# Mixture-of-experts groups: VectorE turns squares two groups ahead, TensorE turns the first group, and gates are chosen in front of outputs

## The chip, the cores and the metric

The kernel runs on one core of a Trainium2 chip. The metric is the device time of one execution in microseconds, the median of several. A core has TensorE for matrix products, VectorE, ScalarE and GpSimd for everything else on chip, and SyncE, which here does nothing but issue transfers. The profile calls them PE, DVE, ACT, POOL and SP, and TensorE's loading of a stationary operand PEld. Each engine has its own list of instructions and works through it in order; engines wait for each other by semaphores.

## The reference

All numbers are fp32. A graph layer (a 4096 by 4096 adjacency matrix times features) is followed by a causal attention layer with four heads of 64, and then by the experts, which are what the change touches:

```python
x = x + y @ wo.T
flat = _rmsnorm(x, ln2_w).reshape(-1, Cx)            # 4096 tokens of 256
probs = jax.nn.softmax(flat @ router_w.T, axis=-1)   # 8 experts
tp, ti = jax.lax.top_k(probs, TOPK)                  # 2 for each token
tp = tp / (jnp.sum(tp, axis=-1, keepdims=True) + 1e-09)
weights = jnp.sum(tp[..., None] * jax.nn.one_hot(ti, NE, dtype=flat.dtype), axis=1)
out = jnp.zeros_like(flat)
for e in range(NE):
    hh = jax.nn.silu(flat @ w1[e].T) * (flat @ w3[e].T)   # 682 hidden units
    out = out + weights[:, e:e + 1] * (hh @ w2[e].T)
return x + out.reshape(Bx, Tx, Cx)
```

## The kernel before, in words

The graph layer takes the first third of the span and attention the second. While attention still runs, a router picks two experts for each token and writes the token's row (normalised values, its place in the output, its gates) into lists in DRAM, one stretch for each expert. The expert stage starts at about 1027 us. It works through 42 groups of listed tokens, each belonging to one expert. A group is *whole* (256 tokens) or *small* (128 tokens). `TURNS` gives the order: turns 0 to 8 are whole; from 9 on small and whole mostly alternate, but small follows small at turns 15 and 16, 24 and 25, 31 and 32, and a whole one comes behind each of these pairs; the last two turns are whole.

**Inputs.** TensorE needs the tokens with their 256 features on partitions, so the listed rows must be transposed. `load_squares(k)` (issues at L1426) does part of that by DMA: four transfers, one for each quarter of the partitions, put 32 by 32 squares in place. `prepare(k)` does the rest: VectorE transposes inside squares (L1443), and ScalarE scales by the norm's weights into `xT` (L1448, one instruction for each half of the features). VectorE then also forms four sums of the inputs for a group that needs them (`sums_x`, L1512), and picks the gate of each token from its row (L1455 and L1460), which came by a transfer of its own (`load_rows`, L1433).

**Products.** For a small group, and for whole groups up to turn 10, `hidden` forms the hidden units in steps of `q`: products (L1728), silu on ScalarE (L1734), multiplication on VectorE (L1735). After the first step it calls `prepare` for the next turn. For whole groups from turn 12 to 39, `hidden_seven` forms the same in the manner of Strassen, with seven products of half-sized blocks in place of eight (L1558). Its banks A, B and D of PSUM are copied out by ScalarE (L1564) and added to by VectorE (L1567), first for most chunks (`one`), then for the rest (`two`); a bank that was just copied is written again by a later product, S2 by T2 after S1 by T1. It calls `prepare` for the next turn near its end, and then multiplies (L1596 and L1597) and forms sums of the hidden units (`split`, L1645 to L1648). The sums of its input weights are made by GpSimd in the turn before (`sums13`, L1491 to L1494 and on).

**Outputs.** `combine(k)` runs one turn late, inside turn k + 1 and behind that turn's hidden units. It multiplies by the second weight matrix: plainly for small groups (L1779), by seven products for whole groups from turn 4 on (`seven_products`, L1688), which need sums of the weights (`sums2`, L1664 to L1667, on VectorE; made ahead where a whole group follows a small one) and a recombination on VectorE (L1696 to L1702). ScalarE multiplies by the gate (L1790), and GpSimd adds the rows into the output by an indirect transfer (L1801).

**What sets the order.** The loop over turns is written out by hand: hidden units of k; sums of weights for k + 1 if due; outputs of k − 1; then GpSimd sets `sent` (L1937) and SP writes it to DRAM (L1938), which holds SP's queue behind the outputs; then SP issues `load2(k + 4)` (L1403), `load13(k + 5)` (L1397), the squares and the rows of k + 4. Loads of the first groups are issued from inside attention (`begin_experts`), and `prepare(0)` stands in the list of attention's last steps, before its last value products (L827) and beside its last row sums (L813).

Of the kernel before, what the change touches and what calls it, by code (L numbers as in the profile page):

```python
# [66 lines left out]
def fast_kernel(  # L67
# [618 lines left out]
    with (  # L686
# [668 lines left out]
        def entry(t, most):  # L1355
            return nc.values_load(
                t, engines=[SP], min_val=0, max_val=most,
                skip_runtime_bounds_check_because="the lists are as long as the tokens are many",
            )
# [25 lines left out]
            at2 += (pt_all[:, at + 2 * W13 : at + 2 * W13 + W2],)  # L1385
        w13s = [a.rearrange("p (c w) -> p c w", c=2) for a in at13]
        w2s = [a.rearrange("p (k c) -> p k c", k=NF + 1) for a in at2]
        rows, hidden_of, inputs_of, expert_of, gates_of, rows_at = {}, {}, {}, {}, {}, {}


        def halves(i):
            return HALF if i < NW else 1

        def load13(k):
            i = TURNS[k]
            expert_of[i] = entry(table[0:1, 1, i : i + 1], NE - 1)
            nc.sync.dma_start(  # L1397
                w13s[k % 5], w13[bass.ds(expert_of[i], 1)].rearrange("o p c w -> p (o c) w")
            )
# [8 lines left out]
        def loaded(i, get):  # L1408
            if i < NA:
                free(get, "late writes", "the rows of the first groups are whole by then")  # L1410
                join(get, "first reads")

        def squares_room(k):
            return late[:, LATE_Z + k % 5 * 2 * C : LATE_Z + (k % 5 + 1) * 2 * C]

        def load_squares(k):

            i = TURNS[k]
            n = halves(i)
            at = rows_at[i] = entry(  # L1420
                table[0:1, 0, i : i + 1], NE * REG - (GR if i < NW else 0)
            )
            z = squares_room(k)[:, 0 : n * C].rearrange("p (m e) -> p m e", e=2 * Q)
            tokens = lists[bass.ds(at, n * P), 0:C].rearrange("(m i) (g e) -> g i m e", i=Q, g=4)
            for g in range(4):
                loaded(i, nc.sync.dma_start(z[g * Q : (g + 1) * Q], tokens[g]))  # L1426

# [8 lines left out]
            ))  # L1436
            rows[i] = r

        def prepare(k):
            i = TURNS[k]  # L1440
            n = halves(i)
            turned = squares_room(k + 4)[:, 0 : n * C]
            nc.vector.transpose(turned, squares_room(k)[:, 0 : n * C])  # L1443
            turned = turned.rearrange("p (m c i) -> p c m i", c=2, i=Q)
            xT = late[:, LATE_XT + k % 2 * 2 * GR : LATE_XT + k % 2 * 2 * GR + 2 * n * P]
            xT = xT.rearrange("p (c i) -> p c i", c=2)
            for c in range(2):
                nc.scalar.activation(  # L1448
                    xT[:, c, :].rearrange("p (m i) -> p m i", i=Q), turned[:, c], AF.Copy, scale=ln2_sb[:, c : c + 1]
                )  # L1450
            inputs_of[i] = xT
            if k in SPLIT13:
                sums_x(k, turned)
            pick = ex.tile([P, n, NE], F32, tag="pick", name=f"pick_{i}")
            nc.vector.tensor_mul(  # L1455
                pick, rows[i][:, 0:n, 1:KEPT],
                mine[:, i : i + 1, :].to_broadcast([P, n, NE]),
            )
            gates_of[i] = ex.tile([P, n, 1], F32, tag="gt", name=f"gt_{i}", bufs=3)
            nc.vector.tensor_reduce(gates_of[i], pick, AX.X, ALU.add)  # L1460

# [57 lines left out]
        def hidden_seven(k, step, behind):  # L1519
# [46 lines left out]
            def added(dst, q, bank):  # L1566
                nc.vector.tensor_add(dst, dst, bank[:, 0 : len(q.chunks), :])  # L1567
# [10 lines left out]
                copied(q.u2, q, q.A)  # L1578
                product(q, q.D, "S4", "B22")

            def added_up(q):
                added(q.s1, q, q.B)
                added(q.u2, q, q.D)

            def third(q):
# [15 lines left out]
            sums2(k)  # L1601
            begun(one)
            second(one)
            added_up(one)
            step()
            begun(two)
            third(one)
# [9 lines left out]
            third(two)  # L1617
            step()
            if behind is not None:
                prepare(behind)  # L1620
            gated(two)
            si = ax.tile([P, GR], F32, tag="rden", name=f"si_{i}_t")
            nc.scalar.activation(si[T0 : T0 + TAIL, :], tail[0:TAIL, :], AF.Silu)
# [81 lines left out]
        def hidden(k, step=None, behind=None):  # L1705
            i = TURNS[k]
            n = halves(i) * P
            w13_sb, xT = w13s[k % 5], inputs_of.pop(i)
            hT = hTs[k % 2][:, :, 0:n]
            for q in range(0, NF + 1, 2):  # L1710
                if not p_h:
                    pool = next(p_sc)
                    if pool is p_sc1:
                        ps = [
                            pool.tile([P, 2, GR], F32, tag="sc", name=f"h_{i}_{q}_{m}")
                            for m in range(2)
                        ]
                    else:
                        ps = pool.tile([P, 2, 2, GR], F32, tag="sc", name=f"h_{i}_{q}")
                        ps = [ps[:, m] for m in range(2)]  # L1720
                else:
                    ps = [
                        p_h[0].tile([P, 2, GR], F32, tag="h", name=f"h_{i}_{q}_{m}")[:, :, 0:n]
                        for m in range(2)
                    ]
                for m in range(2 * q, min(2 * q + 4, 2 * NF + 1)):
                    for c in range(2):
                        nc.tensor.matmul(  # L1728
                            ps[m % 2][:, m // 2 - q, :], w13_sb[:, c, m * P : (m + 1) * P],
                            xT[:, c, :], start=(c == 0), stop=(c == 1),  # L1730
                        )
# [3 lines left out]
                nc.vector.tensor_mul(  # L1735
                    hT[:, q : q + both, :], si[:, 0:both, :], ps[1][:, 0:both, :]
                )
                if q == 0 and behind is not None:
                    prepare(behind)
                if step and q < NF - 1:  # L1740
                    step()

            nc.scalar.activation(si[T0 : T0 + TAIL, 1, :], ps[0][0:TAIL, 1, :], AF.Silu)
            nc.vector.tensor_mul(
                hT[T0 : T0 + TAIL, NF, :], si[T0 : T0 + TAIL, 1, :], ps[0][T0 : T0 + TAIL, 1, :]
            )
            hidden_of[i] = hT
            if k in SEVEN:
                split(k, hT)

        def combine(k):
# [2 lines left out]
            w2_sb = w2s[k % 5]  # L1754
            hT = hidden_of.pop(i)
            r = rows.pop(i)
            gt = gates_of.pop(i)
            if k < ALONE or k % 2:
                y = ax.tile([P, HALF, C], F32, tag="yT1", name=f"y_{i}")
            else:  # L1760
# [52 lines left out]

        def begin_experts():
            make_table(NB - 1, True, 0, NA)
            load13(0)
            load_squares(0)
            load_squares(1)
            load2(0)
            load13(1)  # L1820
            for k in range(2):
                load_rows(k)
            load_squares(2)
            load2(1)
            load_squares(3)
            for k in range(2, 4):
                load_rows(k)
# [39 lines left out]
        for b in ORDER[:-1]:  # L1867
# [7 lines left out]
            lambda: give_back([("late", n) for n in range(4)])  # L1875
        )
        later.setdefault(PLACES - 2, []).append(
            lambda: [prepare(0)] + [nc.gpsimd.memset(t[:, NF, :], 0.0) for t in hTs]
        )

        scored = 0
# [31 lines left out]
        load13(3)  # L1913
        load2(3)
        load13(4)
        for k in range(NM):
            if k == 3:
                sc_scope.close()
                p_h.append(ctx_h.enter_context(tc.tile_pool(name="e_h", bufs=6, space=PSUM)))
            if k == NM - 1:  # L1920


                between = iter([lambda: None, lambda: combine(k - 1)])
            if k in SPLIT13:
                hidden_seven(k, step, k + 1)
            else:
                hidden(
                    k, step if k < NM - 1 else lambda: next(between)(),
                    k + 1 if k + 1 < NM else None,
                )  # L1930
            step()
            if k + 1 in SPLIT13 and TURNS[k] >= NW:
                sums2(k + 1)
            if 0 < k < NM - 1:
                combine(k - 1)
                if k + 4 < NM:
                    nc.gpsimd.memset(sent, 0.0)  # L1937
                    nc.sync.dma_start(sent_dram, sent)  # L1938
            if k + 4 < NM:
                load2(k + 4)  # L1940
            if k + 5 < NM:
                load13(k + 5)
            if k + 4 < NM:
                load_squares(k + 4)
                load_rows(k + 4)
            if 0 < k < NM - 1:
                step()
                if k >= ALONE and TURNS[k - 1] < NW:
# [746 lines left out]
```

## Time and profile before

| | us |
|---|---|
| median of 3 runs | 1547.53 (1547.2 to 1548.44) |
| profiled execution, device time | 1541.6 |
| its span | 1539.8 |
| adjacency and attention products in it, L532 and L785 | 370.4 and 282.3 busy |
| first expert product | at 1032.0 |
| mean granted TensorE clock | 0.997 |

The span is what the profiler saw from the first to the last instruction. The profiled execution lies 5.9 us below the median, so places in it are compared among themselves, and differences, not totals, are carried over to the median. A wait is listed by the engine that waited, its line, what released it, and then total us, number, and longest. In a timeline line the first number is the start in us, the second the length, and brackets hold the idle time of the engine just before and what ended it; lengths of consecutive equal instructions are lumped and their number given as x.

Times of single operations, as far as the change touches them, all from the same execution:

| operation | us each |
|---|---|
| turn, L1443, small and whole | 0.44 and 0.70 |
| scaling, L1448, two of a small and two of a whole group | 0.69 and 0.91 |
| pick, L1455, mean of 42 (alone: 0.17) | 0.466 |
| gate, L1460, mean | 0.166 |
| one input sum, L1512, mean | 0.50 to 0.58 |
| small output, L1790 | 0.47 |

### The profile page before, as it was taken

Reading aid. Unit: us, or ns where it says so; the run is one execution under the profiler, and the core shown is the slowest. Engines: PE = TensorE matmul, PEld = TensorE weight load, DVE = VectorE, ACT = ScalarE, POOL = GpSimd, SP = SyncE. Lnnn points to the kernel's source line nnn. Section 1 sums busy time; section 2 is a strip of 40 time slices with the busy share of each in tenths; the row PEclk is TensorE's granted clock in tenths of the full one; section 3 lists DMA queues with packets and bytes.
Section 4 is the critical chain, followed back from the end, with each engine's and each line's share of the span. In section 5 each row is a group of like instructions: output and inputs, shape, how many; then the busy total and the mean of one; then the engine's idle time right before and its main releaser. Section 6 shows DMA issues by size and latency. Waiting matters only on the chain.

```text
span 1539.8 us, 28601 instructions
## 1 busy us (share of the span) xinstructions
PE 1509.4 (98%) x10791; PEld 1113.9 (72%) x10791; DVE 1085.2 (70%) x2224; ACT 554.4 (36%) x989; POOL 556.6 (36%) x649
## 2 busy tenths in 40 slices
PE   9999999999999999999999999989999999999987
PEld 8888888888888543444444434448899899999986
DVE  7864665755655667878878978875676787787872
ACT  2102012021021456565665565643123333333331
POOL 2102022122221331374554643442424545545342
PEclk9999999999999999999999999999999999999999
DMA  6344444543544000011011011059878798898955
GB/s 239 131 132 153 154 140 147 173 146 124 174 142 149 5 1 29 15 58 36 29 51 36 33 33 37 22 164 293 221 213 229 225 271 242 234 282 232 265 118 133
DMA packets 106590, 212.19 MB, mean 138 GB/s; under 512 B 63466, under 2 KB 82922, under 8 KB 92810
## 3 DMA queue, kind: packets, MB, share of 16 engines
q1 hardware_dynamic: 92906, 192.00, 38.7%
q0 software_dynamic: 12720, 17.47, 6.4%
q8 instruction: 87, 1.43, 0.4%
q10 hardware_dynamic: 816, 0.79, 0.2%
q14 instruction: 61, 0.50, 0.1%
HBM read 184.48 MB, written 27.13 MB: 137 GB/s over the span
## 4 chain that ended last, share of the span: by engine, by line
PE 93%; DMA 2%; DVE 2%; issue 1%; POOL 1%; ACT 0%; SPq 0%; DVEq 0%; POOLq 0%; ACTq 0%
PE acc L532 25%; PE sc L785 14%; PE h L1728 13%; PE y_second L827 5%; PE y_third L827 4%; PE y_first L827 4%; PE ye_y L1779 4%; PE hA L1558 4%; PE ye_y L1688 3%; PE ye_ms L1688 2%; PE pq L612 2%; PE pf L503 2%; PE hD L1558 2%; PE ph L193 2%; PE po L913 1%
## 5 line engine op out<-in xcount | busy, mean ns | idle before, releaser
L785 PE MATMUL sc<-qT_all,kT 64*64 64x512 f32 (+3 forms) x2304 | 282.3, 557 | 0.5 <-ACT pt_all L793 0.3
L532 PE MATMUL acc<-a,g 128*128 128x256 f32 x1024 | 244.1, 380 | 0.0
L532 PEld LDWEIGHTS acc<-a,g 128*128 128x128 f32 x1024 | 193.9, 190 | 31.5 <-issue 6.7
L785 PEld LDWEIGHTS sc<-qT_all,kT 64*64 64x64 f32 x2304 | 91.3, 133 | 128.5 <-issue 109.1
L793 ACT ACTIVATE pt_all<-sc 128x1024 f32<-128x1024 f32 (+3 forms) x157 | 148.7, 954 | 96.8 <-PE sc L785 94.4
L1801 POOL DMA_INDIRECT acc_dram<-y,late x40 | 63.1, 1577 | 185.0 <-ACT y L1790 121.3
L532 PE MATMUL acc<-more_sums,g 128*128 128x256 f32 x512 | 126.3, 380 | 0.0
L813 DVE TENSOR_TENSOR late<-late,pt_all 128x1024 f32<-128x1024 f32 (+3 forms) x91 | 106.7, 1173 | 24.3 <-POOL pt_all L795 9.9
L1728 PE MATMUL h<-late,qT_all 128*128 128x256 f32 (+1 forms) x616 | 106.7, 333 | 4.6 <-ACT late L1448 4.6
L433 ACT COPY qT_all<-tr 128x512 f32<-128x512 f32 x30 | 16.2, 588 | 259.5 <-PE tr L431 259.5
L532 PEld LDWEIGHTS acc<-more_sums,g 128*128 128x128 f32 x512 | 97.4, 190 | 13.0
L827 PE MATMUL y_first<-pt_all,vv 64*64 64x512 f32 (+3 forms) x448 | 106.6, 554 | 0.0
L1728 PEld LDWEIGHTS h<-late,qT_all 128*128 128x128 f32 x616 | 95.4, 194 | 15.0 <-ACT late L1448 5.4
L625 POOL TENSOR_TENSOR rot<-rot,tables 128x512 f32<-128x512 f32 x21 | 34.1, 1626 | 198.6 <-ACT rot L621 158.4
L827 PE MATMUL y_second<-pt_all,vv 64*64 64x512 f32 (+3 forms) x436 | 104.2, 555 | 0.0
L1075 POOL DMA_INDIRECT lists<-row,slots x64 | 88.3, 1379 | 17.6 <-issue 15.1
L827 PE MATMUL y_third<-pt_all,vv 64*64 64x512 f32 (+3 forms) x372 | 88.8, 555 | 0.0
L621 ACT ACTIVATE rot<-pq 32x512 f32<-32x512 f32 x84 | 49.4, 588 | 82.7 <-DVE qT_all L619 43.7
L1735 DVE TENSOR_TENSOR late<-si,h 128x256 f32<-128x256 f32 (+2 forms) x87 | 39.0, 465 | 56.9 <-ACT si L1734 38.8
L1734 ACT ACTIVATE si<-h 128x256 f32<-128x256 f32 (+2 forms) x87 | 34.7, 413 | 93.2 <-PE h L1728 90.4
L813 DVE TENSOR_TENSOR sum_all<-sum_all,pt_all 128x1024 f32<-128x1024 f32 (+3 forms) x51 | 56.0, 1098 | 15.8 <-POOL pt_all L795 9.5
L793 ACT ACTIVATE late<-sc 128x1024 f32<-128x1024 f32 (+3 forms) x55 | 50.9, 927 | 41.4 <-PE sc L785 38.0
(489 smaller groups left out, 3347.0 us busy)
## 6 DMA issues: line engine op xcount, KB each, us to landing
a<-in_adj_dram SPq DMA_DIRECT2D x64, 1024.0 KB, 4.9
qT_all<-in_w_dram SPq DMA_DIRECT2D x18, 1408.0 KB, 10.0
pt_all<-in_w_dram SPq DMA_DIRECT2D x16, 1408.0 KB
res_all<-in_w_dram SPq DMA_DIRECT2D x17, 768.0 KB, 5.5
pt_all<-in_w_dram SPq DMA_DIRECT2D x16, 768.0 KB, 5.5
res_all<-in_w_dram SPq DMA_DIRECT2D x8, 1408.0 KB, 6.2
qT_all<-in_w_dram SPq DMA_DIRECT2D x9, 768.0 KB, 5.5
late<-lists SPq DMA_DIRECT2D x100, 64.0 KB, 8.7
```

The source lines that it names most:

```text
L532: nc.tensor.matmul(acc[bank][:, at, :], g[jb][:, right, k, :], m[left][:, k, :], start=(jb == 0 and k == 0 and at == 0), stop=(jb == NB - ...
L621: nc.scalar.activation(rot[n * Q : (n + 1) * Q, :], pj[(n ^ 1) * Q : ((n ^ 1) + 1) * Q, :], AF.Copy, scale=1.0 if n % 2 else -1.0,)
L785: nc.tensor.matmul(ps[k * HP : (k + 1) * HP, j, :w], kT[sb][hd, i * P + k * HP : i * P + (k + 1) * HP], qT[b][hd, p, off:], start=True, st ...
L793: nc.scalar.activation(pt[:, :, :w], ps[:, :, :w], AF.Exp, scale=HD ** -0.5)
L813: nc.vector.tensor_add(sums[b, p][:, :, off:], before[:, :, off:], pt[:, :, : 512 - off])
L827: nc.tensor.matmul(accs[b, p][k][hd, off:], vv[sb][some, i, hd], pt[some, j, : 512 - off], start=(s == order_of(b)[0]), stop=(s == order_o ...
L1075: put = nc.gpsimd.indirect_dma_start(out=lists[:, :], out_offset=bass.IndirectOffsetOnAxis(ap=chosen[b][:, k, t, :], axis=0), in_=flats[b] ...
L1558: nc.tensor.matmul(bank[:, n, :], m[left][:, c, :], m[right], start=first and n == 0, stop=True, skip_group_check=True,)
L1688: nc.tensor.matmul(p[number], m[left][:, j, :], m[right][:, j, :], start=(n % 4 == 0 and j == 0), stop=(j == 2), skip_group_check=True,)
L1728: nc.tensor.matmul(ps[m % 2][:, m // 2 - q, :], w13_sb[:, c, m * P : (m + 1) * P], xT[:, c, :], start=(c == 0), stop=(c == 1),)
L1779: nc.tensor.matmul(ps[h if last else 0][:, h, :], hT[:, q, cols], w2_sb[:, q, :], start=(q == 0), stop=(q == NF),)
L1801: put = nc.gpsimd.indirect_dma_start(out=(acc_dram if k < NM - LAST else out)[:, :], out_offset=at, in_=y[:, h, :], in_offset=None, comput ...
```

## The change

Three edits, and what follows from them.

First, the inputs of turn 0. `load_tokens(0)` fetches the 256 rows in one transfer of whole rows, ahead of the first weights on SP. `begin_inputs` takes the place of `prepare(0)`: ScalarE reorders each half of the tokens, TensorE transposes four 128 by 128 blocks into a PSUM bank, and ScalarE scales these into `xT`.

Second, `prepare` is taken apart. `turn(k)` is VectorE's transpose; `turns_in` lists in which turn each is done. A whole group turns the squares of the next turn and, if that is small, those of the turn after it too. In `hidden_seven` the first stands before VectorE's first bank addition of `one` and the second between its two; in `hidden` they stand after the first step. Only where small follows small does a small group turn for its successor. `scale_inputs(k)` is ScalarE's part; a small group whose successor is already turned does it at its very start. Squares are loaded one turn earlier, and those of turn 4 ahead of the loop.

Third, picking the gates moves out of `prepare(k)` into the start of `combine(k)`, in front of the output that it scales. On VectorE it so stands behind the split and the weight sums of the turn in which the outputs are formed.

```diff
+        def load_tokens(k):
+            n = halves(TURNS[k])
+            get = nc.sync.dma_start(
+                squares_room(k)[:, 0 : n * C].rearrange("p (h c) -> p h c", c=C),
+                lists[bass.ds(place_of(TURNS[k]), n * P), 0:C].rearrange(
+                    "(h p) c -> p h c", p=P
+                ),
+            )
+            loaded(TURNS[k], get)
...
-        def prepare(k):
+        def begin_inputs():
+            n = halves(TURNS[0])
+            listed, tokens = (
+                squares_room(at)[:, 0 : n * C].rearrange("p (h c) -> p h c", c=C)
+                for at in (0, 4)
+            )
+            for h in range(n):
+                nc.scalar.copy(in_groups(tokens[:, h]), in_order(listed[:, h]))
+            tr = p_ms.tile([P, 2, n, P], F32, tag="ms", name="tx")
+            for h in range(n):
+                for c in range(2):
+                    nc.tensor.transpose(
+                        tr[:, c, h, :], tokens[:, h, c * P : (c + 1) * P], ident
+                    )
+            xT = room_for_inputs(0)
+            for c in range(2):
+                nc.scalar.activation(
+                    xT[:, c, :], tr[:, c].rearrange("p h i -> p (h i)"), AF.Copy,
+                    scale=ln2_sb[:, c : c + 1],
+                )
+
+        turned_of, turns_in = {}, {}
+        for k in range(1, NM):
+            alone = TURNS[k - 1] < NW or TURNS[k - 2] >= NW
+            turns_in.setdefault(k - 1 if alone else k - 2, []).append(k)
+
+        def turn(k):
+            n = halves(TURNS[k])
+            turned = squares_room(k + 4)[:, 0 : n * C]
+            nc.vector.transpose(turned, squares_room(k)[:, 0 : n * C])
+            turned_of[k] = turned.rearrange("p (m c i) -> p c m i", c=2, i=Q)
...
+        def gates(k, r):
...
-            def added_up(q):
+            def added_up(q, behind=()):
+                behind = iter(behind)
+                for j in behind:
+                    turn(j)
+                    break
                 added(q.s1, q, q.B)
+                for j in behind:
+                    turn(j)
                 added(q.u2, q, q.D)
...
-            added_up(one)
+            added_up(one, turns_in.pop(k, []))
...
-                prepare(behind)
+                scale_inputs(behind)
+                if behind in SPLIT13:
+                    sums_x(behind, turned_of.pop(behind))
...
+            early = behind in turned_of
+            if early:
+                scale_inputs(behind)
             for q in range(0, NF + 1, 2):
...
                 if q == 0 and behind is not None:
-                    prepare(behind)
+                    for j in turns_in.pop(k, []):
+                        turn(j)
+                    if not early:
+                        scale_inputs(behind)
+                    if behind in SPLIT13:
+                        sums_x(behind, turned_of.pop(behind))
...
-            gt = gates_of.pop(i)
+            gt = gates(k, r)
...
+            load_tokens(0)
             load13(0)
-            load_squares(0)
             load_squares(1)
...
-            lambda: [prepare(0)] + [nc.gpsimd.memset(t[:, NF, :], 0.0) for t in hTs]
+            lambda: [begin_inputs()] + [nc.gpsimd.memset(t[:, NF, :], 0.0) for t in hTs]
...
+        load_squares(4)
...
             if k + 4 < NM:
-                load_squares(k + 4)
+                if k + 5 < NM:
+                    load_squares(k + 5)
                 load_rows(k + 4)
```

More of the change, by code (lines that the diff above doesn't have):

```diff
@@ L1387, in fast_kernel @@
         w2s = [a.rearrange("p (k c) -> p k c", k=NF + 1) for a in at2]
-        rows, hidden_of, inputs_of, expert_of, gates_of, rows_at = {}, {}, {}, {}, {}, {}
+        rows, hidden_of, inputs_of, expert_of, rows_at = {}, {}, {}, {}, {}
         def halves(i):
@@ L1414, in squares_room, with place_of @@
             return late[:, LATE_Z + k % 5 * 2 * C : LATE_Z + (k % 5 + 1) * 2 * C]
+        def place_of(i):
+            if i not in rows_at:
+                rows_at[i] = entry(
+                    table[0:1, 0, i : i + 1], NE * REG - (GR if i < NW else 0)
+                )
+            return rows_at[i]
+        def load_tokens(k):
[7 more added lines that the diff above has]
+            loaded(TURNS[k], get)
         def load_squares(k):
@@ L1419, in load_squares @@
             n = halves(i)
-            at = rows_at[i] = entry(
-                table[0:1, 0, i : i + 1], NE * REG - (GR if i < NW else 0)
-            )
-            z = squares_room(k)[:, 0 : n * C].rearrange("p (m e) -> p m e", e=2 * Q)
-            tokens = lists[bass.ds(at, n * P), 0:C].rearrange("(m i) (g e) -> g i m e", i=Q, g=4)
+            z = squares_room(k)[:, 0 : n * C].rearrange("p (m e) -> p m e", e=2 * Q)
+            tokens = lists[bass.ds(place_of(i), n * P), 0:C].rearrange(
+                "(m i) (g e) -> g i m e", i=Q, g=4
+            )
             for g in range(4):
@@ L1437, in load_rows, with room_for_inputs @@
             rows[i] = r
-        def prepare(k):
+        def room_for_inputs(k):
+            n = halves(TURNS[k])
+            xT = late[:, LATE_XT + k % 2 * 2 * GR : LATE_XT + k % 2 * 2 * GR + 2 * n * P]
+            inputs_of[TURNS[k]] = xT.rearrange("p (c i) -> p c i", c=2)
+            return inputs_of[TURNS[k]]
+        def begin_inputs():
[17 more added lines that the diff above has]
+                    scale=ln2_sb[:, c : c + 1],
+                )
@@ new lines, in fast_kernel, with scale_inputs @@
+        turned_of, turns_in = {}, {}
[3 more added lines that the diff above has]
+        def turn(k):
+            n = halves(TURNS[k])
+            turned = squares_room(k + 4)[:, 0 : n * C]
+            nc.vector.transpose(turned, squares_room(k)[:, 0 : n * C])
+            turned_of[k] = turned.rearrange("p (m c i) -> p c m i", c=2, i=Q)
+        def scale_inputs(k):
+            xT = room_for_inputs(k)
+            for c in range(2):
+                nc.scalar.activation(
+                    xT[:, c, :].rearrange("p (m i) -> p m i", i=Q), turned_of[k][:, c],
+                    AF.Copy, scale=ln2_sb[:, c : c + 1],
+                )
@@ L1440, in prepare @@
+        def gates(k, r):
             i = TURNS[k]
             n = halves(i)
[L1442 to L1450, printed above, removed]
@@ L1451, in prepare @@
-            inputs_of[i] = xT
-            if k in SPLIT13:
-                sums_x(k, turned)
             pick = ex.tile([P, n, NE], F32, tag="pick", name=f"pick_{i}")
             nc.vector.tensor_mul(
-                pick, rows[i][:, 0:n, 1:KEPT],
+                pick, r[:, 0:n, 1:KEPT],
                 mine[:, i : i + 1, :].to_broadcast([P, n, NE]),
             )
-            gates_of[i] = ex.tile([P, n, 1], F32, tag="gt", name=f"gt_{i}", bufs=3)
-            nc.vector.tensor_reduce(gates_of[i], pick, AX.X, ALU.add)
+            gt = ex.tile([P, n, 1], F32, tag="gt", name=f"gt_{i}", bufs=3)
@@ L1465, in fast_kernel @@
+            nc.vector.tensor_reduce(gt, pick, AX.X, ALU.add)
+            return gt
         SEVEN = [k for k in range(4, NM - 2) if TURNS[k] < NW]
```

## The prediction

> **What bounds the kernel now.** I read the head of the page first, then its chain of work that ended last.
>
> ```profile
> span 1539.8 us, 28601 instructions
> PE 1509.4 (98%) x10791; PEld 1113.9 (72%) x10791; DVE 1085.2 (70%) x2224; ACT 554.4 (36%) x989; POOL 556.6 (36%) x649
> PE 93%; DMA 2%; DVE 2%; issue 1%; POOL 1%; ACT 0%; SPq 0%; DVEq 0%; POOLq 0%; ACTq 0%
> ```
>
> TensorE is busy 98% of the span. The diff adds four TensorE instructions and takes none away, so it can win only by filling TensorE's gaps. The view of waits, for TensorE from 1000 us on, lists them:
>
> ```profile
> PE hA L1558 <- issue: 12.6, 7, 2.1
> PE h L1728 <- ACT late L1448: 4.6, 1, 4.6
> PE hA L1558 <- DVE hy L1567: 1.2, 1, 1.2
> ```
>
> That is 18.4 us in nine gaps: one of 4.6 at the first expert group, eight of 1.2 to 2.1 later. The timeline at the first:
>
> ```profile
> 1026.87 0.60 PE L827 MATMUL y_second<-pt_all,vv 64*64 64x512 f32 x2
> ...
> 1029.05 1.75 DVE L813 TENSOR_TENSOR sum_all<-sum_all,pt_all 128x256 f32<-128x256 f32 x2
> ...
> 1030.72 0.70 DVE L1443 STREAM_TRANSPOSE late<-late 128x512 f32<-128x512 f32 x1
> 1031.46 0.91 ACT L1448 ACTIVATE late<-late,ln_sb 128x256 f32<-128x256 f32 x2 [6.73 <-DVE late L1443]
> ...
> 1032.02 6.42 PE L1728 MATMUL h<-late,qT_all 128*128 128x256 f32 x16 [4.56 <-ACT late L1448]
> ```
>
> The inputs wait for VectorE's turn, and that stands behind attention's last sums. The windows give, after the times, busy us of PE, PEld, DVE, ACT, POOL, then granted clock, DMA share and GB/s:
>
> ```profile
> 1032.00:1034.00 2.00, 1.98 (x5) 1.61 (x6) 0.00 (x0) 1.98 (x3) 0.00 (x0) 0.50 0.98 366
> 1034.00:1036.00 2.00, 2.00 (x6) 1.56 (x5) 0.00 (x0) 0.14 (x1) 0.00 (x0) 0.50 1.28 168
> 1050.00:1100.00 50.00, 50.00 (x235) 44.08 (x234) 23.53 (x76) 14.69 (x33) 24.75 (x40) 1.00 0.86 248
> 1200.00:1250.00 50.00, 47.93 (x386) 46.68 (x387) 37.33 (x85) 18.50 (x48) 28.13 (x30) 1.00 0.81 223
> ```
>
> After the long gap TensorE runs at half clock until about 1037; the early whole groups then have no gap at all; the mixed stretch has short ones. One of those, group 14 (whole) behind 13 (small):
>
> ```profile
> 1206.05 1.49 DVE L1455 TENSOR_TENSOR pick<-late,mine 128x8 f32<-128x8 f32 x1
> ...
> 1213.61 0.42 DVE L1735 TENSOR_TENSOR late<-si,h 128x256 f32<-128x256 f32 x1
> ...
> 1221.26 0.29 DVE L1700 TENSOR_TENSOR vv<-vv,ye_ms 128x128 f32<-128x128 f32 x1
> ...
> 1221.58 1.02 ACT L1790 ACTIVATE wo_sb<-vv,gt 128x256 f32<-128x256 f32 x2 [4.78 <-DVE vv L1700]
> 1222.51 0.57 ACT L1564 COPY qT_all<-hA 128x512 f32<-128x512 f32 x1
> 1223.18 1.13 PE L1558 MATMUL hA<-kT,res_all 128*128 128x128 f32 x8 [1.99 <-issue]
> ```
>
> The releaser reads "issue", but the order on ScalarE tells it: the copy of bank A (1222.51) is queued behind an output (1221.58) that waits for VectorE's recombination, and the next product into A cannot start before it. VectorE's chain, not TensorE, sets the pace of such a pair: 23.1 us between equal points where it stalls, 20.87 where it does not.
>
> [...] 0.50 after 4.56 us idle, 1.00 after gaps of 2.0. [...] The pick above takes 1.49 us beside GpSimd's weight sums and 0.17 away from them; the transpose keeps 0.44 beside them.
>
> **The change part by part.** *Start.* Removed: four loads of squares and the 0.70 turn behind VectorE's sums. Added: one token load, two ScalarE copies, four TensorE transposes. The token load goes to SP ahead of group 0's w13. I expect tokens by 1023. ScalarE's last exponential ends at 1024.73; two copies of about 0.42 (from the scale, half of 0.91) end at 1025.6. The transposes stand before the last value products. No such row exists; [...] fp32 128x128 products here follow each other at 0.11. I take 0.16 each, 0.66 in all [...]. They and the last products end by 1027.6, and ScalarE's scaling by 1027.6. w13(0), issued 1.2 us later, should land near 1027.5 instead of 1026.2; it could be 1028.7 if the token load is held by the last scatter. First product at 1027.8 instead of 1032.0: −4.2. [...] sixteen products take 3.45 (as a warm set at 1046.71) instead of 6.42: −2.97. The denominators' products need sum_all (1030.8), which TensorE reaches at 1031.2: covered; w13(1) lands at 1037 to 1039, needed at 1039.3: covered, just. I allow +0.2. **Start −7.0** (−4 to −7.5).
>
> *Turns moved.* A whole group now turns one or two squares (0.44 and 0.70) where VectorE idles, 1.05 and 1.51 us by its waits, before and between its bank additions. Those gaps are the cover; without it each turn costs its own length. Squares are loaded one turn earlier: still four issues per group on SP, in the same place of its order (ahead of the rows, behind w13), with one set more up front, behind w13(4). The DMA share of 0.8 leaves room, and the rooms rewritten were read a group before, so I cost it at nothing. In small groups ScalarE's scaling moves to the start. *Gates moved.* Pick and gate (0.34 when undisturbed) move behind split and stand ahead of the outputs that wait on them. No row is new.
>
> For a contended pair I count from the end of the second bank additions, H. Before: 7.84 to the first gated product, 7.94 more to the recombination that frees ScalarE, total 15.78. After: split ends at 6.4, since pick (1.49) is gone from before it, gates 0.37, small output 0.47, scaling 0.86, silu 0.36, so the gated product comes at 8.66 (+0.8, the added wait: the output and all behind it on ScalarE now queue for gates); then no turn and no wait for scaling, 6.69, total 15.35. Gain 0.43. Six such pairs: −2.6. In 33 to 35 the trace also has the 1.2 of hy, and there −2.1 comes out. In group 12 the output of 9 goes behind split and sums: +0.95.
>
> *Small behind small, before a whole group* (turns 15 16 17, 24 25 26, 31 32 33). Here the new wait may bite. The first small output now waits for gates behind VectorE's sums for the next whole group, which GpSimd blocks:
>
> ```profile
> 1248.58 1.78 DVE L1665 TENSOR_TENSOR res_all<-res_all 128x384 f32<-128x384 f32 x1
> 1249.18 0.47 ACT L1790 ACTIVATE y<-ye_y,gt 128x256 f32<-128x256 f32 x1 [1.96 <-PE ye_y L1779]
> ```
>
> VectorE's sums end at 1253.99 against a TensorE need at 1251.7, and at 1349.94 and 1424.10 for 1347.1 and 1419.3. If GpSimd's sums stayed where they are, with 1.45 from VectorE's end to TensorE's start, stalls of 3.6, 4.2 and 4.3 to 6.0 follow. But they should not stay: the delayed output (3.7 us at turn 13) delays its scatter, the flag that gates SP, hence the w13 load (last packet 1245.8) whose landing starts GpSimd's sums (1246.50). Near 1250.2 they miss VectorE's, which then end by 1249.8: no stall. The second starts at 1344.7, stall 0 to 0.9; the third at 1416 to 1418, 0 to 3.8. I take 0, 0.4, 1.9: +2.3. Without that cover it is +12 to 14.
>
> **Steady −2.6 − 2.1 + 0.95 + 2.3 = −1.4** (−4.5 to +9). Sum −8.4: the profiled execution's 1541.6 (1539.8 span and 1.8 around it) becomes 1533.2. It lies 5.9 below the median of 1547.53 (1547.2 to 1548.44); carried over, the median becomes 1539.
>
> **The rivals.** *A, slower: GpSimd's sums still hit VectorE's in the three small-small places.* For it: 1.78 against 0.56 in the trace, and the strict queue. Against: the shift just argued. −7 + 12.5 − 3.7 is +1.8; and [...] half of 2.97 to 2.97 each, +3 to +6 in all: 1549 without, up to 1555 with it. It decides once the new stalls exceed the start's 7.0, the pairs' 3.7 and the 3.1 of resolution: 13.8 with the slow clock counted. *B: the start gains less*, because w13(0) queues behind the token load. For it: SP's order. First product at 1029.5 is −2.5 and −3.0 for the clock, less 1.4: −6.9, or −4 where the small-small places take 3 more: 1541 to 1544. *C: VectorE's relief is worth more,* since turns no longer wait and the pairs become TensorE-bound. Up to 13.8 is there: −7 −10 gives 1530. *D: start's gain and stalls cancel:* new stalls of 10 to 12, 1545 to 1549.
>
> **How the numbers follow.** A difference under 0.2% (3.1 us) is about what a measurement cannot tell from none. Forecast (1535 to 1541) 0.38, B 0.20, C 0.15, D 0.13, A 0.14. Faster: the first three and a little of D, 0.75; same 0.12; slower 0.13. Range 1532 to 1550: it leaves out the better half of C and most of A; the forecast's own is 1535 to 1541.
>
> **What would show it.** The first L1728-kind product near 1027.8 at clock 1.00, no 4.6 us gap; the windows of 1050 to 1196 unchanged in length. In pairs, gaps of about 1.6 in place of 2.0. At 15 to 17, 24 to 26, 31 to 33: the first small output's wait names VectorE's gates; VectorE's sums last 0.56 (my case) or 1.78 (rival A), and TensorE gaps of 3.6 or more there prove A. A late w13(0) as releaser of the first product proves B. The forecast fails if GpSimd's sums keep their place, or if a delayed flag makes some w13 load late for TensorE itself.

## The result and the profile after

The changed kernel takes 1535.43 us, the median of its executions, against 1547.37 for the kernel before beside it: a ratio of 0.9916, interval 0.989 to 0.9942. One of its six executions took 2260.88 us at a mean granted clock of 0.654, a slow state that the ratio leaves out. In a second series of comparisons it took 1535.26 against 1545.36, ratio 0.9942 (0.9928 to 0.9955). So the gain is 9 to 13 us; the forecast was 8.4 us, to 1539, and the sign and the range hold. Beside it, the profiled execution went from 1541.6 to 1535.82, only 5.8 us. Why the medians moved more than the two traces is one of the questions below.

The head of the page after:

```profile
span 1534.1 us, 28641 instructions
PE 1509.4 (98%) x10795; PEld 1113.2 (73%) x10795; DVE 1067.1 (70%) x2223; ACT 551.0 (36%) x991; POOL 559.2 (36%) x649
```

TensorE's busy time is the same, 1509.4; it is four instructions richer. The gain is in gaps. The waits of TensorE from 1000 us on, after:

```profile
PE hA L1609 <- issue: 12.5, 10, 4.5
```

The 4.6 at the start is gone. In the mixed stretch the sum looks as before (12.5 against 12.6 + 1.2), but these are other gaps: ten in place of eight, one of 4.5 us. L1609 is the product of `hidden_seven` that was L1558. First the start, in the timeline after:

```profile
1024.05 0.70 ACT L1468 COPY late<-late 128x256 f32<-128x256 f32 x2
...
1025.74 0.66 PE L1472 MATMUL tx<-ident,late 128*128 128x128 f32 x4
...
1026.43 0.84 ACT L1477 ACTIVATE late<-tx,ln_sb 128x256 f32<-128x256 f32 x2 [1.68 <-PE tx L1472]
...
1027.76 3.69 PE L1790 MATMUL h<-late,qT_all 128*128 128x256 f32 x16
```

The first product comes at 1027.76 in place of 1032.02, its set of sixteen takes 3.69 in place of 6.42. The windows (columns as before) have full clock where the kernel before had half:

```profile
1032.00:1034.00 2.00, 2.00 (x11) 1.44 (x8) 1.31 (x2) 0.62 (x3) 0.00 (x0) 1.00 1.24 219
1034.00:1036.00 2.00, 2.00 (x11) 1.76 (x10) 1.13 (x1) 0.84 (x2) 0.00 (x0) 1.00 1.05 257
```

If TensorE's instructions of the two traces are laid side by side in order, from the first expert product on, the changed kernel is 6.99 us ahead after the first set and stays within 0.6 of that to 1193. Then pairs of whole behind small gain, and whole groups behind two small ones lose: 6.4 ahead at turn 12, 9.5 at its best, 1.9 at the least, behind the worst place, and 6.4 at the end. The pair that the prediction showed, 12 to 14, reads now:

```profile
1207.11 0.42 DVE L1797 TENSOR_TENSOR late<-si,h 128x256 f32<-128x256 f32 x1 [1.65 <-ACT si L1796]
...
1213.48 0.29 DVE L1759 TENSOR_TENSOR vv<-vv,ye_ms 128x128 f32<-128x128 f32 x1
...
1213.80 1.03 ACT L1857 ACTIVATE wo_sb<-vv,gt 128x256 f32<-128x256 f32 x2 [3.40 <-DVE vv L1759]
1214.73 0.57 ACT L1615 COPY qT_all<-hA 128x512 f32<-128x512 f32 x1
...
1215.40 1.13 PE L1609 MATMUL hA<-kT,res_all 128*128 128x128 f32 x8 [0.62 <-issue]
```

The order and the releaser are as before: recombination, output, copy, product. But VectorE comes earlier, and the gap is 0.62 in place of 1.99. The worst place is turn 33 behind turns 31 and 32, both small, on VectorE, ScalarE, GpSimd and TensorE:

```profile
1405.65 2.76 PE L1846 MATMUL ye_y<-res_all,late 128*128 128x256 f32 x12
...
1406.86 0.56 DVE L1723 TENSOR_TENSOR vv<-pt_all 128x384 f32<-128x384 f32 x1
1407.45 1.77 DVE L1724 TENSOR_TENSOR pt_all<-pt_all 128x384 f32<-128x384 f32 x1
1409.15 1.89 DVE L1725 TENSOR_TENSOR vv<-pt_all,vv 128x384 f32<-128x384 f32 x1
1411.08 1.77 DVE L1726 TENSOR_TENSOR vv<-vv,pt_all 128x384 f32<-128x384 f32 x1
1412.77 1.49 DVE L1505 TENSOR_TENSOR pick<-late,mine 128x8 f32<-128x8 f32 x1
...
1407.02 1.79 POOL L1542 TENSOR_TENSOR sum_all<-qT_all 128x640 f32<-128x640 f32 x1 [1.21 <-DMA qT_all<-in_w_dram]
...
1414.54 0.47 ACT L1857 ACTIVATE y<-ye_y,gt 128x256 f32<-128x256 f32 x1 [8.06 <-issue]
...
1415.59 2.05 PE L1609 MATMUL hA<-kT,res_all 128*128 128x128 f32 x8 [4.50 <-issue]
```

The first small output, whose products ended on TensorE at 1408.4, waits 6 us more for its gate; the pick stands behind the sums for turn 33 (L1723 to L1726). The first of these had begun before GpSimd's sums, which start at 1407.02; the other three and the pick run beside them, and these four instructions of 0.16 to 0.56 us take 1.49 to 1.89. TensorE stops for 4.50, and its next products run at half clock (2.05 for eight that took 1.13 in the pair above).

### The profile page after: what moved, and what is told of

Read it like the earlier page. It is cut to its first block, busy times and chain, and to the rows that moved or that the text cites. A ratio compares the mean times of both kernels' runs of the same rounds, so it can differ in the third digit from the quotient of the medians.

```text
span 1534.1 us, 28641 instructions
## 1 busy us (share of the span) xinstructions
PE 1509.4 (98%) x10795; PEld 1113.2 (73%) x10795; DVE 1067.1 (70%) x2223; ACT 551.0 (36%) x991; POOL 559.2 (36%) x649
## 3 DMA queue, kind: packets, MB, share of 16 engines
q8 instruction: 87, 1.43, 0.4%
## 5 line engine op out<-in xcount | busy, mean ns | idle before, releaser
L532 PE MATMUL acc<-qT_all,g 128*128 128x256 f32 x256 | 65.7, 379 | 0.0
```

Source lines behind the costliest of these rows:

```text
L532: nc.tensor.matmul(acc[bank][:, at, :], g[jb][:, right, k, :], m[left][:, k, :], start=(jb == 0 and k == 0 and at == 0), stop=(jb == NB - ...
```

## The experiments

The theory after the comparison: the start gives 7.0, the pairs gain because the turns left VectorE's late queue and ScalarE's wait, and the gates' place costs what the small-small places lose. The rivals: the pairs gain by the gates; the small-small gaps come from GpSimd's weights, not from the gates; the start is worth more, or less, than its trace shows. The first four kernels ran beside one another.

**The kernel before as it is.** Nothing is edited.

> The kernel before, unchanged, to see how far its executions and its gaps differ. Expected ratio to itself 1.000, within 0.2%. The profiled execution of before (1541.6) lay 5.9 us under the median of its other runs. If that was chance, this profile has the same eight gaps of 13.8 us in all from 1150 us on, at 1540 to 1548; if executions differ in their gaps, the gaps listed here are other ones, and 5 us more of them where the time is 5 us longer.

Measured 1544.73 (1539.55 to 1547.92), ratio 0.9998 (0.9986 to 1.001). Its trace has the same eight gaps within 0.04 us, and it still is 1.4 us longer from the first expert product on. All of the difference is behind the last gap, the windows of this trace:

```profile
1486.00:1489.00 3.00, 0.99 (x6) 0.83 (x6) 1.75 (x5) 1.98 (x4) 1.48 (x2) 0.88 0.00 0
1489.00:1492.00 3.00, 3.00 (x17) 3.00 (x17) 0.00 (x0) 0.59 (x1) 1.86 (x4) 0.55 0.60 58
1492.00:1495.00 3.00, 3.00 (x25) 2.90 (x25) 1.42 (x3) 1.69 (x4) 0.00 (x0) 1.00 0.21 30
```

A gap of 2.01 us was followed by half clock here, and the equal gap in the other trace was not. Each execution's mean granted clock is on record: among 35 of the kernel before it runs from 0.992 to 0.997, and the three executions at 0.997 take 1540.9 on average, the seven at 0.993 1547.7. The trace that the prediction was made from is one of 0.997. So neither stated branch was right: the gaps do not differ between executions, the number of half-clock stretches behind them does, and that trace was one of the luckier ones.

What goes with such a stretch can be read from the traces. In the first trace of the kernel before, the record of the granted clock begins, at full clock, at 6.70 us, and the clock changes 1024.00, 1030.83 and 1529.17 us after that; in the first one of the changed kernel it begins at 7.09, and the clock changes 1406.29, 1413.12 and 1522.35 us after. All six are whole multiples of 3.4133 us to within 0.02 (300, 302, 448, 412, 414 and 446 steps). On a grid of such steps the gap above, first in this trace and then in the one that the prediction was made from:

```profile
1484.89:1488.30 3.41, 1.43 (x13) 1.24 (x12) 2.09 (x9) 1.55 (x4) 0.78 (x1) 1.00 0.00 0
1488.30:1491.72 3.42, 3.38 (x16) 3.42 (x17) 0.65 (x1) 1.01 (x2) 2.56 (x4) 0.50 0.45 44
```

```profile
1484.67:1488.08 3.41, 1.82 (x17) 1.63 (x15) 2.44 (x8) 1.17 (x3) 0.40 (x1) 1.00 0.00 0
1488.08:1491.50 3.42, 3.01 (x27) 3.04 (x28) 1.37 (x2) 1.88 (x5) 2.94 (x4) 1.00 0.33 38
```

Here the whole gap lies in one step, TensorE is busy for 0.42 of it, and the next step has half clock. There 0.41 us of the gap lie in the next step, the busy share is 0.53, and the clock stays full. The first traces of the two kernels agree: of their 278 full-clock steps between 1020 and 1505 us two were followed by half clock, that of the start's gap (busy share 0.05) and that of the changed kernel's gap of 4.50 us (0.33); the other 276 have shares of 0.47 and more. So in this place the luck went with where the gap fell on this grid; that it does so in the executions without a trace was not shown.

**The first group alone,** on the kernel before:

```diff
-            load_squares(0)
+            load_tokens(0)          # ahead of load13(0)
...
-            lambda: [prepare(0)] + [...]
+            lambda: [begin_inputs()] + [...]
...
-            gt = gates_of.pop(i)
+            gt = gates_of.pop(k) if k else gates(k, r)
```

> The kernel before with the first group's change alone: token load, copies, TensorE transposes; turns and gates stay where they were (only turn 0's gates are chosen in its outputs). Theory (start 7.0, the rest about zero in sum): 1540.4, first expert product at 1027.8 at full clock, the eight later gaps unchanged at about 13.8 us. Rival (the start is worth all of the 12 us seen in the medians): 1535.5.

Measured 1540.81 against 1545.79, ratio 0.9977 (0.9965 to 0.9988): 3.6 us by the ratio, 5.0 by the medians. The first product is at 1028.33 at full clock. Part of the missing gain is in the waits of TensorE in this trace:

```profile
PE hA L1608 <- issue: 12.4, 7, 2.0
PE hA L1608 <- DVE hy L1617: 2.5, 2, 1.2
PE po L913 <- DVE yT L849: 1.2, 1, 1.2
```

The output projection of attention's last block waits 1.2 us for VectorE's reciprocals, and one more gap of 1.25 has come at turn 26; two half-clock stretches of 3.41 us behind gaps of a pair, which the first trace of before lacks, cost this one 1.6 each. After its first set this trace was 6.4 ahead of that one, and it ends only 0.2 ahead. The rival that all 12 us are in the start falls.

**The small-small edit,** on the changed kernel: the first small output's gates are chosen ahead of the sums.

```diff
             if k + 1 in SPLIT13 and TURNS[k] >= NW:
+                gates_ahead(k - 1)      # gates_of[k - 1] = gates(...), if that turn is small
                 sums2(k + 1)
...
-            gt = gates(k, r)
+            gt = gates_of.pop(k) if k in gates_of else gates(k, r)
```

> The changed kernel with one edit: where small follows small ahead of a whole group, the first one's gates are chosen ahead of the sums of the second weights. Theory (the gaps of 0.75, 1.95 and 4.50 us and some 1.7 us at half clock in these places come from gates queued behind those sums): 8.9 us less than the changed kernel, 1526.5, none of the three gaps left. Rival 1 (GpSimd's weight sums come earlier again, and hold something else): about 3 us less, 1532, gaps of 1 us or more remain there. Rival 2 (the gaps come from late weights on GpSimd): no change, 1535.4.

Measured 1526.19, ratio 0.9883 (0.9863 to 0.9902); the highest of five executions is 1527.38. TensorE's waits:

```profile
PE hA L1614 <- issue: 5.3, 7, 1.4
PE h L1795 <- DMA qT_all<-in_w_dram: 0.4, 1, 0.4
```

All three small-small gaps are gone, seven others stay as they were, and the trace has no half clock in the experts before 1517 us. That is what the theory said, to 0.3 us; both rivals fall.

**The gates put back,** on the changed kernel: the third edit undone, turn 0 excepted.

```diff
                 scale_inputs(behind)
                 if behind in SPLIT13:
                     sums_x(behind, turned_of.pop(behind))
+                gates_of[behind] = gates(behind, rows[TURNS[behind]])
...
-            gt = gates(k, r)
+            gt = gates_of.pop(k) if k else gates(k, r)
```

> The changed kernel with its third edit undone: gates are chosen where a group's inputs are made, as before (turn 0's stay with its outputs). Theory (the pairs gain from the turns that left VectorE's queue and ScalarE's wait, not from the gates): pairs keep gaps of 0.5 to 1.0 us, small-small gaps are gone, 1526 to 1529. Rival (the pairs gained because the pick of gates left the stretch in which GpSimd's sums block VectorE): pairs are back at 1.8 to 2.1 us a gap, 9 us more there and 9 less in small-small, 1535 to 1536.

Measured 1527.06 (1521.61 to 1529.49), ratio 0.989 (0.987 to 0.9909). The waits of its trace:

```profile
PE hA L1609 <- DVE hy L1618: 1.1, 3, 0.6
PE po L913 <- DVE yT L849: 1.0, 1, 1.0
PE h L1791 <- DMA qT_all<-in_w_dram: 0.6, 1, 0.6
```

No gap is left in any pair, although the pick is back in the contended stretch. So the pairs gain by the second edit, and the gates' new place costs them 0.5 to 0.9 each on top of the small-small places. The parts of the second edit (transposes moved, squares loaded a turn earlier, scaling at a small group's start) were not run apart. Late squares were not what held the pairs before: in that trace VectorE sat idle ahead of none of its 42 transposes (L1443). The profiled execution is this kernel's fastest; what its slower ones lose is not traced and stays open.

**The gates alone,** on the kernel before: turns and first group as they were, `gates` called in `combine`.

> The kernel before with its gates alone moved in front of outputs; first group and turns as before. Theory (in pairs the pick gone from the contended stretch is worth little, since the pairs gain by the turns; in small-small the gates stand behind the sums and cost gaps of some 7 us and the slow clock): pairs keep gaps of 1.5 to 2 us, three new gaps in small-small, 5 to 9 us slower than before, 1551 to 1555. Rival (the gates are what relieves the pairs, and the small-small gaps came with the turns and the earlier loads): pairs under 1 us, no new gaps, 1537 to 1540.

Measured 1556.34 against 1545.97, ratio 1.0065 (1.0041 to 1.0089): slower by 6 to 14 us. The waits of its trace:

```profile
PE hA L1608 <- issue: 25.5, 13, 3.3
PE h L1790 <- ACT late L1495: 4.5, 1, 4.5
```

The small-small gaps are 3.30, 3.30 and 3.31, the pairs stand at 2.16 to 2.18, and three half-clock stretches of 3.41 us follow gaps. The theory's sign and places hold; pairs and total are somewhat worse than its numbers.

**Gates ahead of everything,** on the changed kernel: besides the small-small edit, `gates_ahead(k - 1)` stands in front of `split` too.

> The changed kernel with the gates of all small groups chosen ahead of the split and of the weight sums. Theory (what is left in the pairs, gaps of 0.55 to 0.90, and 1.41 behind turns 9 and 10, comes from gates behind split): these gaps are under 0.3, so 5 us less than with the small-small edit alone, 1521. Rival (the pick is back beside GpSimd's sums and blocks VectorE by 1.3 us, which sets the recombination): pair gaps as with that edit or longer, 1526 or more.

Measured 1522.7 (1521.4 to 1525.67), ratio 0.9852 (0.9828 to 0.9876). The waits:

```profile
PE hA L1614 <- DVE hy L1623: 2.5, 3, 1.2
PE h L1796 <- DMA qT_all<-in_w_dram: 0.4, 1, 0.4
```

The pair gaps and the 1.41 behind turns 9 and 10 are gone; what is left are three small ones in small-small places, where VectorE's bank additions come late. It beats both kernels.

**The gates put back, but not turn 1's:** as in the experiment that puts the gates back, with `k > 1` in place of `k`.

> The changed kernel with its gates where they were before, except those of turns 0 and 1, which are chosen with their outputs. Theory (with the gates of turn 1 in the first turn, VectorE waits there for a row load, which delays its reciprocals and costs TensorE 1.0 us at the products of the output projection): that gap is at most 0.3, and the time 1 us below the version with only turn 0's there, 1526. Rival (that gap is hidden by what follows): 1527, no change.

Measured 1525.04 (1520.53 to 1526.91), ratio 0.986 (0.9834 to 0.9886). The gap of 1.0 at the output projection is gone, so the row load of turn 1 was its cause. The time cannot be told from 1527.06 by these intervals, nor from the kernel with gates ahead of everything, beside which it ran. Its trace also shows a gap of 2.2 in one small-small place, with 3.41 us of half clock behind it.

**A filler in the first gap,** on the kernel before, in two sizes; its results are read by nothing.

```diff
         load13(4)
+        warm = p_ms.tile([P, 2, HALF, P], F32, tag="ms", name="warm")
+        for n in range(36):                  # 18 in the second kernel
+            nc.tensor.matmul(warm[:, 0, 0, :], ident, ident, start=True, stop=True)
         for k in range(NM):
```

> The kernel before with 36 products of the identity by itself, into an unused bank, set on TensorE into its gap ahead of the first expert group (about 4 us of work whose results nothing reads). Theory (of the start's 7.0 us, 2.97 are the slow clock that the gap brings): the first expert product still at 1032.0, but at clock 1.00, its sixteen products in 3.5 to 3.7 in place of 6.4, and 1542.8, 3.0 less than before. Rival (the slow clock is off the path, since VectorE's reciprocals wait for the first gates at 1037.8 anyway): no change, with a new gap of about 3 us at the products that need them.

The filler was too long: 36 products are 72 instructions of TensorE and took 8.30 us. The first expert product came at 1035.46, its set took 3.62. Measured 1548.43, ratio 1.0006 (0.9993 to 1.0019). That the slow clock costs 2.8 us of TensorE's time is shown; whether it costs the kernel anything is not, hence the second size.

> The filler of the gap ahead of the first expert group again, with 18 products in place of 36, since 36 took 8.3 us and pushed the first expert product to 1035.5. Theory: 18 take 4.1 us and end before 1032; first product at 1032.0, its set of sixteen in 3.6 in place of 6.4, 2.8 us less than before: 1543. Rival (those 2.8 us come back as a wait for VectorE's reciprocals): no change, 1546, a gap of 2 to 3 us at the output projection's products.

Measured 1546.59 against 1545.36, ratio 1.001 (0.9998 to 1.0022): no gain. The filler took 4.29, the first product is at 1031.96, the set takes 3.72, and then, on TensorE and VectorE:

```profile
1045.58 1.25 PE L913 MATMUL po<-wo_sb,yT 128*128 128x264 f32 x2 [2.20 <-DVE yT L849]
...
1037.81 0.17 DVE L1455 TENSOR_TENSOR pick<-late,mine 128x16 f32<-128x16 f32 x1 [6.44 <-DMA late<-lists]
...
1041.44 3.35 DVE L848 RECIPROCAL rden<-rden 128x512 f32<-128x512 f32 x1 [1.18 <-ACT rden L847]
```

The rival was right: VectorE is held by turn 0's pick until 1037.81, so the reciprocals end late, and most of the clock's gain comes back as a wait of 2.20, behind which this trace has 3.41 us of half clock. In the kernel before, the slow clock is off the path; in the changed one it counts only because the picks of turns 0 and 1 no longer hold VectorE there.

**The changed kernel again, and without its first edit,** beside each other.

> The changed kernel again, for a firmer median beside the two that follow and a second trace of its gaps. Theory: 1535, with the gaps of the first trace (0.75, 1.95 and 4.50 us in small-small, under 1 in pairs), and the half clock after the 4.50 us gap in most executions.

Measured 1535.26 (1532.32 to 1536.77). The pairs are within 0.03 of the first trace. The small-small gaps are 2.02, 0.74 and 3.29 in place of 0.75, 1.95 and 4.50: each place takes one of four values, 1.2 to 1.3 us apart. In these traces one lengthened VectorE instruction stands ahead of a gap of 0.75, two ahead of 1.95 or 2.02, three ahead of 3.29, four ahead of 4.50. No half clock followed the 3.29 in this trace.

> The changed kernel with its first edit undone: turn 0's squares are loaded and turned by VectorE as before. Theory (the start is worth what its trace shows, 7.0 us, inside the changed kernel): 1542.4, first product near 1031 to 1032 at half clock. Rival (it is worth only the 3.6 to 5.0 us that it brought alone, since later work gives the rest back): 1539 to 1540.4.

Measured 1539.88 (1533.0 to 1546.57), ratio 0.9963 (0.9953 to 0.9974) against 0.9942 for the whole change: the first edit is worth 3 to 5 us inside it, not 7. The trace has the first product at 1031.51, at half clock, and is 6 us behind the repeated trace of the changed kernel after the first sets. Its first small-small place has no gap, where that one lost 2.02; its third has 4.51 and half clock behind it, where that one lost 3.29, and at the end the two traces are 7.6 apart. So the rival's number holds for the median and the theory's for this pair of traces. That the small-small places differ from trace to trace by more than the disputed 2 to 4 us is shown; where an earlier start gives part of its gain back in the median stays open.

## Why the prediction was right, point by point

**The start, −7.0: right in the trace.** 6.99 in the comparison of traces; transposes 0.66 for 0.66 estimated, first product 1027.76 for 1027.8, its set of sixteen, estimated at full clock from a warm set, 3.69 for 3.45. Two reservations. The clock's 2.97 was added as though TensorE were free to use it; the filler shows that this needs VectorE free of the early picks, which the gates' move gives. And the edit's worth in the median is 3 to 5.

**The pairs, −3.7 with turns 12 and 33 to 35: right mechanism, size too small.** The six pairs gained 1.37, 1.28, 1.36, 0.94, 1.58 and 1.37, in all 7.9 instead of 2.6. The mis-sized term is the chain's first half: the gated product was set at 8.66 after the second bank additions, and it is at 7.75 (1207.11 against 1199.36): the split ended 5.82 after these additions in place of 6.4, and the steps from there to the product took 1.93 in place of 2.26. For the split the working took off the pick's 1.49; but turn and gate had left the stretch too, and its first bank multiplication began 1.96 earlier (1199.28 is 0.08 ahead of the additions' end, and 1207.65 before was 1.88 behind it). The stretch behind that start is as long as it was, 5.90 for 5.93: the multiplication took 0.75 for 1.91, since it now began ahead of GpSimd's next sum (1199.56), but two later instructions of VectorE were longer by 0.57 each beside GpSimd (L1653, 0.85 for 0.28, and L1704, 1.13 for 0.56). The second half was set at 6.69 and is 6.66. The gap of 1.24 in 33 to 35 vanished (2.1 set), and turn 12 lost 0.59 (0.95 set). Sum −8.6. That the gates were worth nothing here, and even cost, is what putting them back showed; the wait that the working priced at +0.8 is seen as VectorE's idle 1.65 ahead of the gated product.

**Small behind small, +2.3: the step that failed.** Measured +7.2 of gaps and, from the comparison of traces, 1.7 at half clock: +8.9 in the first trace. The cover was there in part. The delayed output did delay GpSimd's sums, which started at 1241.74, 1334.58 and 1407.02, but not by quite enough: taken with the lead that the trace has by then (7.8, 9.5 and 8.4 us), they are 0.6 to 0.7 us ahead of the estimate, in the third place of its early end. The working also asked only that VectorE's sums escape the collision, and left out the pick behind them, which has two inputs in SBUF as well: in the first place it alone was hit, 1.51. The kernel with gates alone has 3.3 in each place, somewhat under the 3.6 to 6.0 worked out without cover. Rival A was thus the right mechanism at rather over half its size (7.2 of gaps for 12.5); the pairs' larger gain paid for it.

**The sum.** −7.0 −8.6 +8.9 is −6.7; the comparison of traces ends 6.4 ahead and the spans differ by 5.7. The forecast's −8.4 is met by two errors of opposite sign, +6.6 and −4.9, so that its nearness is in part luck.

**The trace against the median.** "1.00 after gaps of 2.0" was read off one execution, and taken to hold for all. It does not: the kernel before loses clock behind its 2 us gaps in a varying number of places. The changed kernel has one such gap or two left. Gaps shortened from 2.0 to 0.6 therefore bring more to the median than to a lucky trace. An estimate of how much: a half-clock stretch of 3.41 us takes 0.0011 from the mean clock of such a span (half of 3.41 in 1540), and cost 1.6 us in the unchanged kernel's second trace and twice in that with the start alone. In the second series the mean clock averages 0.9939 over the 35 executions before and 0.9968 over the six after; that is 2.6 stretches, or about 4 us in the medians, while the clocks of the first two traces, 0.997 and 0.996, do not favour the change. That this accounts for the whole 4 to 6 us between traces and medians was not shown.

## What to carry to other kernels

When an instruction is moved to where its result is needed, look at what now stands ahead of it in its engine's order, and at what another engine does beside it: a gate of 0.3 us behind four sums held an output for 6. Here the cure was to choose the gates early enough to be behind nothing, once the transposes were out of the way; the three edits together were worth less than two of them. And before a short gap is called cheap, look at the granted clock of several executions, not of one.

## What the runs showed of the hardware

- A gap of 2.01 us on TensorE was followed by 3.42 us of half clock in one trace of the kernel before, and by full clock in another, at the same place (1486). In steps of 3.41 us, TensorE was busy for 1.43 us (0.42) of the step ahead of the loss, and for 1.82 (0.53) of the step where there was none. In the first traces of the two kernels half clock followed full-clock steps with busy shares of 0.05 and 0.33, and none of the 276 with 0.47 or more.
- In the trace after, from 1100 us on, 35 VectorE instructions with two SBUF inputs started while one of GpSimd's sums ran. Each took longer than the shortest of its kind by what was left of that sum less 0.13 to 0.14 us, or by nothing where less than that was left; 74 others with one of the two inputs in PSUM kept their length within 0.02 beside such sums, and five transposes within 0.01. With 1.47 us left the pick of 1412.77 took 1.49 for 0.16, with 1.36 left L1724 of 1407.45 took 1.77 for 0.56, and with 0.7 left L1704 of 1202.27 took 1.13 for 0.56 and L1653 of 1200.74 took 0.85 for 0.28. In the small-small places each lengthened instruction met a new sum 0.2 to 0.5 us after that sum's start, and the gaps come in steps of 1.2 to 1.3.
- In the filler, a 128x128 fp32 product was two instructions of TensorE of 0.115 us each (36 of them: 72, 8.30 us); in the trace after, a transpose of a 128x128 fp32 block was one, and four of them took 0.66 us.
